# Bringing an expert's gathered rows to the places of the block transposes: by way of DRAM, or by 16 direct transfers on the chip

## The chip, the cores and the metric

The kernel runs on one core of one Trainium2 chip. The metric is the device time of one execution in microseconds (us); the times shown are medians of several runs. TensorE (PE) multiplies matrices and loads their weights (PEld), VectorE (DVE), ScalarE (ACT) and GpSimd (POOL) do the rest of the arithmetic, and SyncE (SP) only issues transfers. Sixteen DMA engines carry out the transfers of all queues.

## The reference, cut to what matters

The input is 2048 tokens of 512 numbers (batch 8, sequence 256). A first layer adds to x a long convolution over `ctx` gated by the normalised x. The second layer, where the change lies, is a mixture of experts:

```python
x = hidden_states.reshape(-1, h)                       # 2048 tokens of 512, normalised
scores = softmax(x @ gate_w.T)                         # 16 experts
topk_w, topk_i = top_k(scores, 4)                      # 4 experts a token, weights made to sum to 1
...                                                    # each expert takes at most CAP = 256 tokens
xg = xpad[buf]                                         # (16, 256, 512): every expert's gathered rows
mid = silu(xg @ w_gate) * (xg @ w_up)                  # 512 -> 352
eout = (mid @ w_down) * wbuf                           # 352 -> 512
y = zeros(T + 1, h).at[buf].add(eout)                  # added back to the tokens' rows
shared = silu(x @ sw_gate) * (x @ sw_up) @ sw_down     # 704 wide, for all tokens
out = x + y + shared
```

## The kernel before, in words

All arithmetic is float32. The order of the instructions on each engine is the order in which the Python code writes them; each engine and each queue works in that order. The framework puts in the semaphore waits that the data need.

The first half of the time (to about 340 us) is the convolution layer. Between its steps the kernel places pieces of the shared MLP: `shared_block` is a generator, and `fill(n)` runs its next n pieces on PE. A piece multiplies into a PSUM tile `sgu` (two buffers, tag `mm`); ACT makes `act` of it and DVE multiplies both into `smid` (L179). The last shared blocks run from 357 to 419 us, while the experts' routing is worked out on DVE and POOL.

Then 16 experts run one after the other. For expert e:

- `find` (L915) turns the routing into two lists of 128 row numbers, `ido` to gather by and `idx` to scatter by.
- `gather(e)` (L974) is two indirect DMAs on POOL. They bring 256 rows of `xw_d` (512 numbers and 16 weights each) from DRAM into the tile `g`, laid out [128 partitions, 2 halves of the list, 528]. `g` has two buffers.
- `shuffle(g)` (L985) makes `gb` of `g`. DVE's transpose works on blocks of 32 x 32, so to get the transposed matrix the rows' 32-row groups j and the 128-column groups i have to change places: what stands in partitions 32j to 32j+31 and columns 128i to 128i+127 of `g` is wanted in partitions 32i to 32i+31, at place j of `gb`. The kernel before does that in DRAM: one store of the 512 KB (L989), a wait until it landed, and four fetches of 128 KB (L992), all on SP. `gb` has two buffers.
- `tokens(e)` (L998) copies the weights `wg` out of `g` and transposes `gb` into `xgT` with two DVE instructions (L404).
- `gate_up` (L1023) and `down` (L1076) are the matmuls: 24 groups of gate and up (`pgu`, lines 1034, 1046, 1054), then for each half of the list the down projection (`eo`, L1080). `down` also scales the result on DVE and adds it to `out` by an indirect DMA on POOL (L1091).
- `load_expert` (L852) issues four weight loads on SP, 2112 KB in all.

The experts are prepared three ahead (`AHEAD = 3`). Gathers and shuffles of experts 0, 1 and 2 are issued before the loop, among the last shared blocks. In the loop, `tokens(e + 1)` comes behind the gate and up matmuls of e, and at the end of expert e SP gets the weights and the shuffle of e + 3:

```python
        if e + AHEAD < E:
            experts[e + AHEAD] = load_expert(e + AHEAD)
            moved[e + AHEAD] = shuffle(gathered[e + AHEAD])
```

So SP works through four weight loads and one shuffle for each expert, in this order, and what waits in one of them holds up all behind it. SP also carries the stores of `out` (L196) that the shared blocks end with.

Of the kernel before, what the change touches and what calls it, by code (L numbers as in the profile page):

```python
# [8 lines left out]
F32 = mybir.dt.float32  # L9
# [11 lines left out]
P = 128  # L21
BK = 32
B, S, L = 8, 256, 512
# [7 lines left out]
E, K, CAP, I, IS = 16, 4, 256, 352, 704  # L31
NSL = CAP // P
NB = P // BK
# [20 lines left out]
def ssm_attention__then__moe_kernel(  # L54
# [22 lines left out]
    nc = tc.nc  # L77
# [7 lines left out]
    dram = ctx.enter_context(tc.tile_pool(name="dram", bufs=1, space=DRAM))  # L85
# [52 lines left out]
    def transpose_blocks(dst, got):  # L138

        nc.vector.transpose(dst, got.rearrange("p j (c f) -> p c j f", f=BK))  # L140
# [119 lines left out]
    with ExitStack() as att:  # L260
# [16 lines left out]
            out=exch,  # L277
            in_=exch,
# [386 lines left out]
        def stir(count):  # L665
# [7 lines left out]
            out=skip_b,  # L673
            in_=bass.AP(tensor=skip.tensor, offset=skip.offset + FIRST * HT, ap=[[0, P], [1, HT]]),
# [164 lines left out]
    ffn = ctx.enter_context(tc.tile_pool(name="ffn", bufs=2))  # L839
# [6 lines left out]
    AHEAD = 3  # L846
# [138 lines left out]
    def shuffle(g):  # L985


        slots = dram.tile([CAP, L], F32, name="slots", bufs=2)
        nc.sync.dma_start(out=slots.rearrange("(n q) f -> q n f", n=NSL), in_=g[:, :, 0:L])  # L989
        gb = ffn.tile([P, NSL * NB, P], F32, name="gb", bufs=AHEAD - 1)  # L990
        for i in range(NB):
            nc.sync.dma_start(  # L992
                out=gb[i * BK : (i + 1) * BK],
                in_=slots[:, i * P : (i + 1) * P].rearrange("(j b) f -> b j f", b=BK),
            )
        return gb

    def tokens(e):  # L998

        gb, g = moved.pop(e), gathered.pop(e)  # L1000
        wg = ffn.tile([P, NSL], F32, name="wg")
        for n in range(NSL):
            nc.vector.tensor_copy(wg[:, n : n + 1], g[:, n, L + e : L + e + 1])
        xgT = ffn.tile([P, NC, CAP], F32, name="xgT")
        for n in range(NSL):
            transpose_blocks(xgT[:, :, n * P : (n + 1) * P], gb[:, n * NB : (n + 1) * NB])
        return xgT, wg

    NW, Q = I // P, P // 4
# [99 lines left out]
    for e in range(AHEAD - 1):  # L1109
        gathered[e] = gather(e)  # L1110
        moved[e] = shuffle(gathered[e])
    fill(6)
    xgT_next = tokens(0)
    wt_next = pack(experts[0][0])
    gathered[AHEAD - 1] = gather(AHEAD - 1)
    moved[AHEAD - 1] = shuffle(gathered[AHEAD - 1])
    while behind:
        fill(1)
    for e in range(E):
        w, wd = experts.pop(e)  # L1120
        wt = wt_next
        xgT, wg = xgT_next
        mid = ffn.tile([P, NI, CAP], F32, name="mid")
        if e + 1 < E:
            gate_up(xgT, mid, w, wt, slice(0, CAP))
            wt_next = pack(experts[e + 1][0])
            xgT_next = tokens(e + 1)
            if e + AHEAD < E:
                find(e + AHEAD, hots.pop(e + AHEAD))
                gathered[e + AHEAD] = gather(e + AHEAD)  # L1130
            for n in range(NSL):
                down(e, n, mid, wd, wg)
            if e + AHEAD + 1 < E:
                hots[e + AHEAD + 1] = compare(e + AHEAD + 1)
        else:

            gate_up(xgT, mid, w, wt, slice(0, P))
            gate_up(xgT, mid, w, wt, slice(P, CAP), (NW,))
            down(e, 0, mid, wd, wg)
            gate_up(xgT, mid, w, wt, slice(P, CAP), range(NW))  # L1140
            down(e, 1, mid, wd, wg)
# [3 lines that stand above are left out]
# [38 lines left out]
```

## Time and profile before

| | |
|---|---|
| median of 3 runs | 678.43 us (678.39 to 678.44) |
| the profiled execution | 678.52 us |
| its span, first to last instruction | 676.8 us |
| mean granted TensorE clock | 0.995 |
| DMA packets | 98439, 117.79 MB |

The span is what the tables of the profile cover; the profiled execution's own time lies 1.7 us over it. A share of busy time tells how full an engine is on average; which wait ends last in a stage has to be read from the chain of waits, the waits and the timeline of that stage. SP's entries are issues: their length is the time that the queue's sequencer took, not that of the transfer.

### The profile page before, as it was taken

The numbers are of one execution on the slowest core, as the hardware profiler recorded it, in microseconds if no ns is written. First come the engines' busy times: TensorE is split into PE (matmuls) and PEld (weight loads), VectorE is DVE, ScalarE is ACT, GpSimd is POOL, SyncE is SP. The second block draws the span as 40 slices with busy tenths as digits, with TensorE's granted clock in tenths as the row PEclk, the third lists the DMA queues.
The fourth block names the chain that finished last, engine by engine and source line by source line (L and its number), as shares of the span: only waits on it lengthen the run. The fifth ranks groups of instructions, "written<-read, shape, count | busy, mean of one in ns | idle before, by whom it ended". The sixth has DMA issues, their size and how long they took to land.

```text
span 676.8 us, 9807 instructions
## 1 busy us (share of the span) xinstructions
PE 654.2 (97%) x3321; PEld 486.9 (72%) x3321; DVE 385.8 (57%) x932; ACT 184.2 (27%) x465; POOL 320.2 (47%) x509
## 2 busy tenths in 40 slices
PE   6899999998999999999999999999999999999994
PEld 5687877777867877876867685777776667777772
DVE  4956576878877776767536621444445545553231
ACT  2464533444342343313332010111121111111110
POOL 5677646877685777547120320243333444443111
PEclk9999999999999999999999999999999999999998
DMA  5793455555557536351008672588888889999822
GB/s 131 237 269 105 125 151 145 145 140 140 147 141 188 134 94 161 103 133 46 16 23 298 198 234 64 169 267 255 259 269 269 256 258 270 271 266 273 248 32 31
DMA packets 98439, 117.79 MB, mean 174 GB/s; under 512 B 11268, under 2 KB 64356, under 8 KB 98389
## 3 DMA queue, kind: packets, MB, share of 16 engines
q1 hardware_dynamic: 90932, 99.86, 48.9%
q0 software_dynamic: 7168, 17.04, 12.1%
q10 hardware_dynamic: 288, 0.26, 0.3%
q8 instruction: 26, 0.43, 0.3%
q14 instruction: 25, 0.20, 0.1%
HBM read 84.25 MB, written 32.88 MB: 173 GB/s over the span
## 4 chain that ended last, share of the span: by engine, by line
PE 85%; DVE 4%; DMA 3%; issue 2%; POOL 2%; ACT 2%; SPq 1%; POOLq 0%; DVEq 0%; ACTq 0%
PE sgu L168 20%; PE pgu L1034 15%; PE y L468 15%; PE eo L1080 12%; PE so L185 11%; PE pgu L1054 4%; PE pgu L1046 2%; PE sgt L154 2%; PE shared L468 2%; PE ip L920 1%; PE pt L529 1%; POOL kv L445 1%; DMA xs<-in_x 1%; DMA out<-eo_sb,idx 1%; DVE y L517 1%
## 5 line engine op out<-in xcount | busy, mean ns | idle before, releaser
L468 PE MATMUL y<-kv,toep 128*128 128x288 f32 x528 | 138.7, 407 | 4.8 <-DVE f L518 3.0
L468 PEld LDWEIGHTS y<-kv,toep 128*128 128x128 f32 x528 | 98.9, 190 | 35.4 <-issue 7.1
L977 POOL DMA_INDIRECT g<-xw_d,ido x32 | 34.9, 1092 | 170.8 <-DVE idx L943 132.3
L520 POOL TENSOR_TENSOR f<-f 128x256 f32<-128x256 f32 x60 | 43.8, 730 | 90.2 <-DVE f L518 85.0
L445 POOL TENSOR_TENSOR kv<-k 128x256 f32<-128x256 f32 x126 | 85.1, 707 | 0.0
L1091 POOL DMA_INDIRECT out<-eo_sb,idx x32 | 59.5, 1859 | 46.1 <-DVE eo_sb L1088 35.4
L168 PE MATMUL sgu<-xnT,swg 128*128 128x256 f32 (+1 forms) x400 | 78.1, 338 | 0.4 <-DVE tail L162 0.4
L1034 PE MATMUL pgu<-xgT,w 128*128 128x256 f32 (+1 forms) x384 | 78.2, 362 | 0.0
L168 PE MATMUL sgu<-xnT,swu 128*128 128x256 f32 (+1 forms) x400 | 77.9, 338 | 0.0
L1034 PEld LDWEIGHTS pgu<-xgT,w 128*128 128x128 f32 x384 | 68.2, 190 | 8.7 <-issue 0.5
L185 PE MATMUL so<-swd,smid 128*128 128x512 f32 x160 | 73.9, 593 | 0.0
L168 PEld LDWEIGHTS sgu<-xnT,swg 128*128 128x128 f32 x400 | 65.3, 191 | 7.9 <-DVE tail L162 0.6
L168 PEld LDWEIGHTS sgu<-xnT,swu 128*128 128x128 f32 x400 | 64.6, 191 | 6.3
L1080 PE MATMUL eo<-wd,mid 96*128 96x512 f32 (+1 forms) x132 | 59.4, 598 | 0.0
L1042 DVE TENSOR_TENSOR mid<-eact,pgu 128x256 f32<-128x256 f32 (+1 forms) x34 | 13.8, 406 | 77.6 <-ACT eact L1041 77.6
L491 DVE TENSOR_TENSOR y<-y,again 128x576 f32<-128x576 f32 x28 | 21.4, 766 | 57.8 <-PE y L468 48.1
L185 PEld LDWEIGHTS so<-swd,smid 128*128 128x128 f32 x160 | 29.9, 190 | 31.9 <-issue 30.4
L177 ACT ACTIVATE act<-sgu 128x256 f32<-128x256 f32 (+1 forms) x50 | 17.1, 341 | 121.6 <-PE sgu L168 121.6
L518 DVE TENSOR_TENSOR f<-y,z 128x512 f32<-128x512 f32 x64 | 44.3, 692 | 6.6 <-DVE y L517 0.5
L517 DVE TENSOR_TENSOR y<-y,q 128x512 f32<-128x512 f32 x64 | 44.8, 700 | 2.2
L1063 ACT ACTIVATE eact<-pgu 32x128 f32<-32x128 f32 x32 | 8.5, 267 | 129.0 <-PE pgu L1054 123.8
L1080 PEld LDWEIGHTS eo<-wd,mid 96*128 96x128 f32 (+1 forms) x132 | 24.1, 189 | 26.0 <-issue 23.5
(178 smaller groups left out, 928.2 us busy)
## 6 DMA issues: line engine op xcount, KB each, us to landing
toep<-win_d SPq DMA_DIRECT2D x28, 320.0 KB
slots<-g SPq DMA_DIRECT2D x16, 512.0 KB
gb<-slots SPq DMA_DIRECT2D x64, 128.0 KB
w<-in_L_ffn_w_gate SPq DMA_DIRECT2D x11, 704.0 KB
w<-in_L_ffn_w_up SPq DMA_DIRECT2D x11, 704.0 KB
got<-sent SPq DMA_DIRECT2D x26, 256.0 KB
wd<-in_L_ffn_w_down SPq DMA_DIRECT2D x11, 512.0 KB
xs<-in_x SPq DMA_DIRECT2D x16, 256.0 KB
```

Of the source, the lines that this page charges most:

```text
L168: nc.tensor.matmul(pgu[:, k, :], lhsT=sw[:, c, f * P : (f + 1) * P], rhs=toks[:, c, :], start=(c == 0), stop=(c == NC - 1),)
L185: nc.tensor.matmul(po, lhsT=m[:, i * P : (i + 1) * P], rhs=swd[:, (f - 1) % (NF + 1), :], start=(f == 0), stop=(f == NF),)
L445: (nc.vector if c in helped else nc.gpsimd).tensor_mul(kv[:, c, 0 : ND * HB].rearrange("p (d w) -> p d w", d=ND), kh[:, c, 0:HB].unsqueeze ...
L468: nc.tensor.matmul(out, lhsT=toep[:, m * P : (m + 1) * P], rhs=rhs, start=(n == 0), stop=(n == len(pairs) - 1),)
L517: nc.vector.tensor_mul(yd, yd, view(qq, 0, [[qc, 2], [B, ND], [1, HB]]))
L518: nc.vector.tensor_add(f, yd, z[:, :, :, BACK : BACK + HB])
L520: adder.tensor_add(f[:, :, 0:2, :], f[:, :, 0:2, :], f[:, :, 2:4, :])
L977: nc.gpsimd.indirect_dma_start(out=g[:, n, :], out_offset=None, in_=xw_d[:, :], in_offset=bass.IndirectOffsetOnAxis(ap=ido[:, e, n : n + 1 ...
L1034: nc.tensor.matmul(pgu[:, k, cols], lhsT=w[:, k, c, f * P : (f + 1) * P], rhs=xgT[:, c, cols], start=(c == 0), stop=(c == NC - 1),)
L1054: nc.tensor.matmul(pgu[:, 0, cols], lhsT=wt[:, c, 0:P], rhs=xgT[:, c, cols], start=(c == 0), stop=(c == NC - 1),)
L1080: nc.tensor.matmul(po, lhsT=mid[:m, f, n * P : (n + 1) * P], rhs=wd[:m, f, :], start=(k == 0), stop=(k == NW),)
L1091: done = nc.gpsimd.indirect_dma_start(out=out, out_offset=bass.IndirectOffsetOnAxis(ap=idx[:, e, n : n + 1], axis=0), in_=o, in_offset=Non ...
```

## The change

`shuffle` no longer makes the tile `slots` in DRAM. For each of the four row groups j and four column groups i it issues one transfer on SP that reads 32 partitions of `g` and writes 32 partitions of `gb`: two runs of 512 bytes for each partition, 32 KB in all. `gb` gets one dimension more, [128, 2, 4, 128] in place of [128, 8, 128], and `tokens` indexes it so. The bytes in `gb` and their places are the same.

```diff
     def shuffle(g):
-        slots = dram.tile([CAP, L], F32, name="slots", bufs=2)
-        nc.sync.dma_start(out=slots.rearrange("(n q) f -> q n f", n=NSL), in_=g[:, :, 0:L])
-        gb = ffn.tile([P, NSL * NB, P], F32, name="gb", bufs=AHEAD - 1)
-        for i in range(NB):
-            nc.sync.dma_start(
-                out=gb[i * BK : (i + 1) * BK],
-                in_=slots[:, i * P : (i + 1) * P].rearrange("(j b) f -> b j f", b=BK),
-            )
+        gb = ffn.tile([P, NSL, NB, P], F32, name="gb", bufs=AHEAD - 1)
+        for j in range(NB):
+            for i in range(NB):
+                nc.sync.dma_start(
+                    out=gb[i * BK : (i + 1) * BK, :, j, :],
+                    in_=g[j * BK : (j + 1) * BK, :, i * P : (i + 1) * P],
+                )
         return gb
...
-            transpose_blocks(xgT[:, :, n * P : (n + 1) * P], gb[:, n * NB : (n + 1) * NB])
+            transpose_blocks(xgT[:, :, n * P : (n + 1) * P], gb[:, n])
```

## The prediction

> **What bounds the kernel now.** I read the page first, for which engine has no idle time left.
>
> ```profile
> span 676.8 us, 9807 instructions
> PE 654.2 (97%) x3321; PEld 486.9 (72%) x3321; DVE 385.8 (57%) x932; ACT 184.2 (27%) x465; POOL 320.2 (47%) x509
> PE   6899999998999999999999999999999999999994
> DMA  5793455555557536351008672588888889999822
> ```
>
> TensorE is full from end to end; but in the last third, where the experts run, the 16 DMA engines stand at 8 and 9 tenths too. So two things can decide: TensorE, and whether data still comes in time. The chain of waits in order of time shows one expert like the next (start, length, step):
>
> ```profile
> 605.28 1.02 PE pgu L1046 x16
> 606.31 1.92 PE pgu L1054 x8
> 608.23 6.91 PE pgu L1034 x32
> 615.52 5.26 PE eo L1080 x12
> 620.78 1.02 PE pgu L1046 x16
> ```
>
> 15.50 us per expert; the 0.38 between 615.14 and 615.52 is `find`'s matmuls, so no step waits. The table of windows agrees: in 605 to 620 PE is busy 15.00 of 15.00 us with the DMA share at 0.94. The waits, of the engines and of SP's queue, say who waits for the code that is replaced:
>
> ```profile
> DVE xgT L404 <- DMA gb<-slots: 1.5, 1, 1.5
> SPq L992 <- DMA slots<-g: 111.3, 15, 11.3
> SPq L860 <- DMA w<-in_L_ffn_w_up: 1.5, 1, 1.5
> ```
>
> The big number, 111.3 us, is SP itself, holding the fetches until the store landed. No compute engine pays for it, save DVE once, 1.5 us before the first expert, and PE did not stop there. The third line is a limit to keep in mind: a weight load at 366.78 waited for the landing of another weight load, issued at 360.38, eight SP transfers earlier. An SP issue waits for the one eight before it.
>
> Last the timeline, at the only place where DVE waited, and through one later cycle of SP:
>
> ```profile
> 390.31 0.38 SPq L989 DMA_DIRECT2D slots<-g  x1
> 393.55 1.81 SPq L992 DMA_DIRECT2D gb<-slots  x4
> 397.69 1.31 DVE L404 STREAM_TRANSPOSE xgT<-gb 128x512 f32<-128x512 f32 x2 [1.49 <-DMA gb<-slots]
> 399.11 0.42 DVE L179 TENSOR_TENSOR smid<-act,sgu 128x256 f32<-128x256 f32 x1
> 401.94 1.89 PE L168 MATMUL sgu<-xnT,swg 128*128 128x256 f32 x8
> ...
> 591.65 0.38 SPq L859 DMA_DIRECT2D w<-in_L_ffn_w_gate  x1
> 592.08 0.43 SPq L860 DMA_DIRECT2D w<-in_L_ffn_w_up  x1
> 592.61 0.43 SPq L861 DMA_DIRECT2D wd<-in_L_ffn_w_down  x1
> 593.08 0.77 SPq L864 DMA_DIRECT2D wd<-in_L_ffn_w_down  x1
> 593.96 0.56 SPq L989 DMA_DIRECT2D slots<-g  x1
> 605.90 1.80 SPq L992 DMA_DIRECT2D gb<-slots  x4
> 607.80 0.48 SPq L859 DMA_DIRECT2D xs<-in_L_ffn_w_gate  x1
> ```
>
> **Own time.** The profiled execution took 678.52 us, 1.7 outside its span of 676.8, and 0.09 over the median 678.43. Changes are added to the median.
>
> **Part 1: what goes.** Per expert one store and four fetches, and SP's wait between them. Compute paid only DVE's 1.5 us, under which PE kept running: worth 0. The waits cannot pay off at the end either: SP's last fetches are issued at 636.37, and from there to PE's end at 667.3 no PE step waits.
>
> **Part 2: what comes, on SP.** 16 issues of 32 KB instead of 5. No row shows a transfer from on-chip memory to on-chip memory. The nearest are 12 transfers of 64 KB in a row, over 32 partitions in 512-byte runs, kp out, got in, qp out: from 124.82 to 130.51, 0.474 us each. Sixteen are 7.6 us. Bounds: 0.40 (the first issues of other groups) and 0.6 (issues of 256 KB), so 6.4 to 9.6; I take 7.6.
>
> **Part 3: on the DMA engines.** In 395 to 397.4 queue q1 used 89.7% of 16 engines for 1069 packets, nearly all 512-byte fetches: 32 ns a packet. In 124.8 to 126.4, kp's stores, 268 packets at 34.0%: also 32 ns. The expert's 1024 pieces thus cost 1024 x 32 / 16 = 2.1 us by either side's row, 4.1 if reading and writing on chip add up. Gone are fetches of 2.1 and the store: 71.3% over 391.5 to 393.6, 1.5 us. So the DMA load of 0.94 x 15.5 = 14.6 us per expert goes to 13.1, or at worst 15.1. Below 15.5 in both cases; I take 13.1, since two rows give the same price.
>
> **Part 4: the first expert.** SP starts at 390.31 (the gathered rows are there), so the 16th issue is at 390.31 + 15 x 0.474 = 397.4. From the last old fetch (393.55 + 3 x 0.474 = 395.0) to DVE's start it was 2.7 us, so DVE starts about 400.1, not 397.69. Queued behind the waiting transposes on DVE is `smid`, the product of a shared block: it frees a PSUM buffer that PE's matmuls at 401.94 need (two buffers). 400.1 + 1.31 + 0.11 + 0.42 = 401.94: just in time. So the cover of about 2.4 us that `smid` had is used up: cost 0 to 0.4, taken 0.2; at an issue pace of 0.6 it is 401.94 + 15 x 0.13 = 1.9 late. Also POOL's gather for expert 2 (396.47) now waits for the reads of `g`, to about 400; its rows are due at 445. The out stores behind on SP (401.03) slip some 5 us; the first scatter on `out` is at 434.86. Moves for experts 1 and 2 end by about 414, in time for the next SP issue at 414.92. All hidden.
>
> **Part 5: the experts in the loop.** SP's cycle: the old one ran (636.37 - 443.05) / 12 = 16.1 us, 0.6 over PE's 15.5. It could, because the first in-loop fetches were issued by 444.88 and due at 461.28: the lead shrank, and is still 8.3 us at the end (638.27, due 646.57). New cycle: weights issued 0 to 2.3, four moves to 4.2, then the eight-back rule holds: moves 5 to 8 follow as the four weight loads land, 9 to 16 as moves 1 to 8 land. Old store and weights drained by 14.25 us (591.65 to 605.90), 13.1 at 607.80. Without the old fetches ahead (2.1, against about 1.0 of late moves) and with 0.5 of moves in place of the store's 1.5, that is about 11 to 12; then 8 x 0.474 = 3.8: a cycle of 15 to 16. Worst, nothing gained: 13.4 + 3.8 = 17.2. The lead allows 461.28 - 2.7 - (437.95 + 7.6) = 13 us over 12 cycles, 1.1 each: break-even is 16.6. I take 15.5 to 16, cost 0.
>
> The rows above show 12 small transfers overlapping at 0.474 us each. The Trainium skill, "DMA: Bandwidth & Descriptors" (Rules for kernel authors), speaks against the change: coalesce small transfers, since under 64 KB one pays mostly overhead, a fixed time that it puts near 2 us for transfers that GpSimd issues. By that price paid in turn, 16 moves would be 32 us, an estimate by which SP's cycle would be twice PE's and the kernel some 200 us slower. The trace does not bear it out where transfers overlap.
>
> Sum: 678.43 + 0 + 0.2 + 0 = 678.6. About 0.2%, 1.36 us, is what a measurement of this kernel can tell from no change.
>
> **Rivals.**
> *SP's cycle becomes the bound (slower).* For it: the eight-back rule, 20 issues where 9 were, a DMA share of 0.94. Against it: less DMA work, and a 13 us lead. Its place is the wait of `xgT` for `gb` in late experts; it decides from a cycle of 16.6. At 17.2: 12 x 1.7 - 13 = 7.4 late, 686.
> *The first expert's moves stall a shared block (slower).* At a pace of 0.6, or one issue held up 1.7 as in fetches at 407.16 (3.06 us for four): 1.4 to 2, so 680.3.
> *It does not do what it says:* pieces for different `j` interleave in the same partitions; were each held behind the last one there, four rounds of about 2.7 would come after the weights: a cycle of 13.4 + 3 x 2.7 = 21.5, 12 x 6 - 13 = 59 late, 737. Against it: `swt`'s two interleaved halves, at 17.36 and 18.01, were issued with no wait between.
> *Faster:* the DMA relief shortens something at the end. But only 668 to 676.8 is free of PE, with no SP transfer near it; at most some tenths through the last scatter, or 1.5 if the first matmuls had stood behind DVE: 677.
>
> **How the numbers follow.** No change 0.56; first-expert stall 0.17; SP's cycle 0.20; ordered pieces 0.03; faster 0.04. Slower is 0.40. The range starts at 678.0, a little under the first case, and ends at 687, past the first-expert stall and past SP's case at 17.2; what it leaves out is the faster case, the ordered one and longer cycles. The likeliest case alone: 678.2 to 679.4.
>
> **What would show it.** Right: in the waits the 111.3 us of SP at the store are gone; PE is 15.00 of 15.00 in windows of the expert stage; the DMA share there falls from 0.94 to about 0.85; DVE's `xgT` waits once, about 4 us, near 396 to 400. Wrong: `xgT L404 <- DMA gb<-g` among DVE's waits for several experts, PE idle at `pgu L1046`, an issue pace over 0.6 or SP's cycle over 16.6.

## The result, and the profile after

The kernel with direct moves takes 679.84 us (median of 20 runs, 678.10 to 680.29) against 678.41 us before (20 runs on the same chip, 678.18 to 678.58). By the medians it is 1.43 us slower, 0.21%; the ratio is 1.0019, with a 95% interval of [1.0012, 1.0026]. That is at the bound of 0.2% that the prediction named, and clear of no change. The profiled execution took 680.24 us, 1.7 outside its span again. Of the 20 times, 17 lie between 679.66 and 680.29 and three between 678.10 and 678.35; the profiled one belongs to the many.

The page, for the same four rows as before:

```profile
span 678.5 us, 10053 instructions
PE 655.6 (97%) x3321; PEld 487.7 (72%) x3321; DVE 386.2 (57%) x932; ACT 184.2 (27%) x465; POOL 319.7 (47%) x509
PE   7899999998999999999999999999999999999994
DMA  5794455555556535441018632677899999999822
```

The span grew by 1.7 us. TensorE is as full as it was, and the DMA row has not become lighter: eight nines in a row where there were four. The waits (total, times, longest):

```profile
PE sgu L168 <- DVE smid L179: 1.4, 1, 1.4
SPq L991 <- DMA g<-xw_d,ido: 11.8, 3, 4.9
DVE xgT L404 <- DMA gb<-g: 5.6, 1, 5.6
```

SP's 111.3 us at the store's landing are gone, as the change promised. The moves wait for their gathered rows only three times, once before the loop (4.4 us) and for experts 3 and 4 in it (2.5 and 4.9). In the loop they also wait for weight loads to land, up to 1.7 us at a time, as the prediction said of transfers issued eight places ahead. In exchange `xgT` waits 5.6 us, once, and there is a wait of TensorE, 1.4 us, that the kernel before did not have. The timeline shows where (SP's 32 issues are those of experts 0 and 1):

```profile
390.26 22.03 SPq L991 DMA_DIRECT2D gb<-g  x32
401.94 1.31 DVE L404 STREAM_TRANSPOSE xgT<-gb 128x512 f32<-128x512 f32 x2 [5.61 <-DMA gb<-g]
403.17 0.71 DVE L179 TENSOR_TENSOR smid<-act,sgu 128x256 f32<-128x256 f32 x2
403.60 1.99 PE L168 MATMUL sgu<-xnT,swg 128*128 128x256 f32 x8 [1.37 <-DVE smid L179]
```

SP begins to issue at 390.26, as before, but expert 0's rows are on their places only at 401.94. DVE stands before the two transposes until then, with `smid` queued behind them. `smid` was done at 399.53 before; here the first is done only near 403.6, and PE, which needed its PSUM buffer at 401.94 in the old trace, stops for 1.37 us. The chain of waits names the same steps, and what comes behind:

```profile
400.08 1.84 DMA gb<-g
401.94 1.31 DVE xgT L404 x2
403.24 0.32 DVE smid L179
403.60 7.17 PE sgu L168 x32
...
421.08 1.02 PE pgu L1045 x16
...
607.04 1.02 PE pgu L1045 x16
...
622.54 1.02 PE pgu L1045 x16
```

The first matmul of expert 0 starts at 421.08, 1.77 us later than before (419.31; 0.12 of this was there at 389.98 already, ahead of the moves), and from there the experts follow at 15.50 us each, as before. So the whole loss arises before 421, and neither the loop nor the end adds to it. In the window 607 to 622 (us, then busy time of PE, PEld, DVE, ACT and POOL, the clock, the DMA share and GB/s) PE has no gap:

```profile
607.00:622.00 15.00, 15.00 (x85) 11.01 (x84) 7.69 (x19) 2.49 (x7) 5.65 (x6) 1.00 0.96 252
```

The DMA engines move 252 GB/s there against 284 before, yet their share is 0.96, not lower than 0.94.

What one issue costs stands in the source view of line 991 (least, median and most, in ns):

```profile
L991 SPq DMA_DIRECT2D gb<-g x256: 585/595/1927, 390.3 to 642.5; - x128
```

About 0.59 us, and 0.04 more to the next: 0.64 a move. Sixteen take 10.4 us (390.26 to 400.67), where the old store, wait and fetches took 5.1.

### The profile page after: what moved, and what is told of

The parts are those of the page before. It is cut to its first block, busy times and chain, and to the rows that moved or that the text cites. A ratio compares the mean times of both kernels' runs of the same rounds, so it can differ in the third digit from the quotient of the medians.

```text
span 678.5 us, 10053 instructions
## 1 busy us (share of the span) xinstructions
PE 655.6 (97%) x3321; PEld 487.7 (72%) x3321; DVE 386.2 (57%) x932; ACT 184.2 (27%) x465; POOL 319.7 (47%) x509
## 2 busy tenths in 40 slices
DMA packets 97160, 109.42 MB, mean 161 GB/s; under 512 B 14084, under 2 KB 67172, under 8 KB 97109
## 3 DMA queue, kind: packets, MB, share of 16 engines
q1 hardware_dynamic: 89652, 91.48, 46.3%
q0 software_dynamic: 7168, 17.04, 14.0%
## 4 chain that ended last, share of the span: by engine, by line
PE 81%; DMA 5%; DVE 4%; POOL 2%; issue 2%; SPq 2%; ACT 2%; POOLq 0%; DVEq 0%; ACTq 0%
PE sgu L168 17%; PE pgu L1033 15%; PE y L468 14%; PE eo L1079 12%; PE so L185 10%; PE pgu L1053 4%; PE pgu L1045 2%; PE shared L468 2%; PE sgt L154 1%; SPq L991 1%; DMA xw_d<-prob 1%; PE pt L529 1%; PE ip L920 1%; POOL kv L445 1%; DMA xs<-in_x 1%
```

## The experiments

My theory: all of the loss is expert 0's 16 moves, which at 0.64 us an issue land after the point where DVE's wait is free. The rival: the loss is a change in the loop or elsewhere on the chip, such as the DMA engines' share, and the wait at 403 only one visible part of it.

### The moves of one expert alone

**first_dram** is after with the old way for expert 0 alone; **first_direct** is before with the moves for expert 0 alone.

```diff
+        if e == 0:          # first_dram; "e > 0" in first_direct
+            slots = dram.tile([CAP, L], F32, name="slots", bufs=2)
+            ...             # the store and four fetches of before
+            return gb
         for j in range(NB):
             for i in range(NB):
```

> After, but expert 0 alone goes by way of DRAM again (one store, four fetches); experts 1 to 15 keep the 16 direct moves. Theory A (the whole 1.4 us is PE's stall at 402 us, where DVE waits for expert 0's moves with smid queued behind it): back to 678.4, within 0.3. Theory B (the cost lies in the loop, in SP's longer cycle or in contention on the DMA engines): stays at 679.8.

> The reverse: expert 0 alone by 16 direct moves, all others by way of DRAM. Theory A: 679.8, the full loss, with PE idle about 1.4 us before L168 at 402 to 404. Theory B: 678.4.

first_dram took 678.27 us (677.95 to 678.44), ratio 0.9998 [0.9989, 1.0007]: the loss is gone, with 240 of 256 moves still there. DVE's timeline:

```profile
398.72 1.30 DVE L404 STREAM_TRANSPOSE xgT<-gb 128x512 f32<-128x512 f32 x2 [2.59 <-DMA gb<-slots]
```

first_direct took 680.21 us (678.40 to 680.37), ratio 1.0023 [1.0014, 1.0032]: 16 moves bring the whole loss, with the same stop of TensorE (timeline, PE):

```profile
403.32 1.99 PE L168 MATMUL sgu<-xnT,swg 128*128 128x256 f32 x8 [1.18 <-DVE smid L179]
```

So in these runs the moves of experts 1 to 15 cost nothing, and those of expert 0 cost everything.

### The same moves with a later due time, or an earlier start

**late_tokens** is after with expert 0's transposes two pieces of the shared block later.

```diff
-    fill(6)
+    fill(8)
     xgT_next = tokens(0)
```

> After, with the transposes of expert 0 placed two pieces of the shared block later on DVE (fill(8) in place of fill(6) before tokens(0)), so that one more smid goes ahead of them. All 16 moves of all experts stay. Theory A: 678.4, since nothing that PE needs is queued behind the wait. Theory B: 679.8.

678.17 us (677.90 to 678.43), ratio 0.9998 [0.9989, 1.0007]. All 256 moves are there; they land no sooner, but `smid` now stands ahead of the transposes in DVE's order (timeline, DVE):

```profile
398.81 0.42 DVE L179 TENSOR_TENSOR smid<-act,sgu 128x256 f32<-128x256 f32 x1 [3.03 <-ACT act L177]
...
401.65 1.30 DVE L404 STREAM_TRANSPOSE xgT<-gb 128x512 f32<-128x512 f32 x2 [2.29 <-DMA gb<-g]
```

The transposes start at 401.65, practically as late as in after, and it costs nothing. What hurt was not their lateness but what stood behind them. The time cannot be told from before's.

**early_prob** lets `prob`'s store, for which the first gather waits, be issued ahead of expert 2's weight loads.

```diff
-    experts = {e: load_expert(e) for e in range(AHEAD)}
+    experts = {e: load_expert(e) for e in range(AHEAD - 1)}
...
     nc.sync.dma_start(out=xw_d[0:T, L:ROW].rearrange("(n q) e -> q n e", q=P), in_=prob)
+    experts[AHEAD - 1] = load_expert(AHEAD - 1)
```

> After, with the weights of expert 2 issued on SP behind the store of prob and not ahead of it, so that prob lands some 6 us earlier and POOL's first gather no longer starts at 382.5 to 383, where it took 2.4 to 2.9 us beside DVE's 2.28 us `hot` (the other gathers: 0.95). Of 20 runs of after 3 took 678.1 to 678.35 and 17 took 679.66 to 680.29. Theory A (the stall at 402 us hangs on when expert 0's rows land; the two kinds of run are a first gather ahead of `hot` or beside it): every run at 678.2 to 678.4, no stall. Rival (the two kinds come from SP's issue pace, whatever the gather does): most runs still at 679.8.

678.15 us (678.03 to 679.38), ratio 0.9996 [0.9988, 1.0005]: gone again. The moves start at 385.81 and the transposes at 397.97, and PE does not stop there. The profiled run is the one at 679.38, and what it has over the other ten comes late in the loop (waits):

```profile
DVE xgT L404 <- DMA gb<-g: 19.9, 7, 3.8
```

Six of the seven waits are those of experts 10 to 15. SP's cycle, from one expert's first weight load to the next, was 16.8 us in this run ((633.72 - 448.73) / 11), over the prediction's break-even of 16.6, and the last experts start 16.00, 15.30 and 15.23 us apart (605.03, 621.03, 636.33, 651.56) where before had 15.50, 15.02 and 15.01: 1.0 us in all. That is the prediction's first rival in small. Why the cycle was longer in this run is open. early_prob also showed something about the gather, to which the last experiments come back.

### What sets the pace of an issue

0.64 lay above my upper bound of 0.6. **pace** adds 32 unused transfers of 32 KB to before, in groups of four: a, chip to chip like a move (32 partitions, two runs of 512 bytes); b, chip to DRAM; c, DRAM to chip; d, chip to chip with one run of 1 KB.

```diff
+    for k, here in enumerate(quarters):
+        nc.sync.dma_start(out=to_a[here], in_=g2[quarters[k - 1], :, 0:P])
+    ...                                        # to_b, to_c, to_d, and all once more
```

> Before, with 32 unused transfers of 32 KB added on SP after the shuffle of expert 2, where SP is idle: four of a kind, twice over. Kinds: a) on chip to on chip, two runs of 512 bytes for each of 32 partitions, like the moves; b) on chip to DRAM, same shape; c) DRAM to on chip, same shape; d) on chip to on chip, one run of 1024 bytes. The moves were issued 0.64 us apart, where 0.474 was expected. If both ends on the chip make the difference: a and d 0.64, b and c 0.47. If the shape with two runs does: a, b and c 0.64, d 0.47. The total says nothing here.

One run, 678.43 us. SP's timeline, four issues a row:

```profile
411.81 2.51 SPq L1127 DMA_DIRECT2D to_b<-g  x4
414.36 2.50 SPq L1130 DMA_DIRECT2D to_c<-xw_d  x4
416.91 2.49 SPq L1132 DMA_DIRECT2D to_d<-g  x4
419.44 2.57 SPq L1125 DMA_DIRECT2D to_a<-g  x4
```

0.63 to 0.64 for all four: neither having both ends on the chip nor having two runs a partition is by itself the reason. Both branches of what I expected fell. **pace2** varies size and runs, all from the chip to DRAM: e, 32 partitions with four runs of 512 bytes, 64 KB; f, 32 with one run of 2 KB; h, 128 with one of 512 bytes; i, 32 with four of 256 bytes, 32 KB; j, 32 with two of 2 KB, 128 KB.

```diff
+        nc.sync.dma_start(out=to_e[k, :, :, 0:P], in_=g2[here, 0, 0:L].rearrange("p (n f) -> p n f", f=P))
+        ...                                    # to_f, to_h, to_i, to_j
```

> Before, with 20 unused transfers from the chip to DRAM added on SP after the shuffle of expert 2, four of a kind: e) 64 KB, 32 partitions with four runs of 512 bytes; f) 64 KB, 32 partitions with one run of 2 KB; h) 64 KB, 128 partitions with one run of 512 bytes; i) 32 KB, 32 partitions with four runs of 256 bytes; j) 128 KB, 32 partitions with two runs of 2 KB. All four kinds of the run pace were issued 0.64 us apart, wherever their ends lay; kp's stores, 64 KB in four runs, 0.474. If size decides: i 0.64, all others 0.47. If the number of runs in a partition decides (four or more are quick): e and i 0.47, f, h and j 0.64. The total says nothing here.

```profile
409.62 2.57 SPq L1125 DMA_DIRECT2D to_e<-g  x4
412.24 1.99 SPq L1127 DMA_DIRECT2D to_f<-g  x4
414.27 1.88 SPq L1129 DMA_DIRECT2D to_h<-g  x4
416.19 2.48 SPq L1131 DMA_DIRECT2D to_i<-g  x4
418.72 2.51 SPq L1133 DMA_DIRECT2D to_j<-g  x4
```

h goes at 0.47 and f does too after its first; e, i and j at 0.63 to 0.64. Size decides nothing: e and h both have 64 KB in runs of 512 bytes. What divides them is how the two ends are described. In e, i, j, b and c the DRAM end runs together into rows of another count than the chip's end (e: 32 x 4 x 128 numbers on the chip, 128 x 128 in DRAM); in f and h both ends have one shape. **pace3** puts that to the test with four kinds of one size, 32 partitions with two runs of 512 bytes: k, chip to DRAM with equal shapes; o, the same with a contiguous DRAM end; l, DRAM to chip with equal shapes; m, chip to chip as in a move.

```diff
+    to_k = dram.tile([NB, NSL, BK, P], F32, name="to_k")
+    to_o = dram.tile([NB, BK, NSL, P], F32, name="to_o")
+        nc.sync.dma_start(out=to_k[k].rearrange("n b f -> b n f"), in_=g2[here, :, 0:P])
+        nc.sync.dma_start(out=to_o[k], in_=g2[here, :, 0:P])
+        ...                                    # to_l, to_m
```

> Before, with 16 unused transfers behind the gather of expert 2, four of each kind, all of 32 KB in 64 runs of 512 bytes over 32 partitions. k: chip to DRAM, both ends described as 32 x 2 x 128; o: the same to a contiguous place, so that the DRAM end is described as 64 x 128 and the two ends differ in shape; l: DRAM to chip, both ends 32 x 2 x 128; m: chip to chip, both ends 32 x 2 x 128, as the changed kernel's moves. Theory (a transfer with one end in DRAM and both ends of one shape is issued quickly, any other slowly; that is how all kinds measured so far divide): k and l 0.43 to 0.48 us per issue, o and m 0.59 to 0.65. Rival (32 partitions with two runs each are slow wherever they go; nothing measured so far had that shape and was quick): all four 0.59 to 0.65. Time of the kernel within 0.2% of before.

```profile
408.12 2.84 SPq L1124 DMA_DIRECT2D to_k<-g  x4
411.01 2.56 SPq L1126 DMA_DIRECT2D to_o<-g  x4
413.61 1.99 SPq L1128 DMA_DIRECT2D to_l<-xw_d  x4
415.65 2.57 SPq L1130 DMA_DIRECT2D to_m<-g  x4
```

The rows of four hide a first issue each: k's first took 1.43 us and its other three 0.43, 0.42 and 0.43; l's first 0.58 and then 0.42, 0.43 and 0.42; o and m 0.59 to 0.65 throughout. For these transfers the theory holds: an issue is quick (0.43, with the gap 0.47) when one end is in DRAM and both are described by the same shape, and slow (0.59, with the gap 0.64) when the shapes differ or both ends are on the chip. The trace's own records of the issues name the rows of the destination, and agree with this reading: 1 x 128 for e and 1 x 64 for o, but 2 x 32 for k, l and m. Why the issue takes longer, the records don't show. k's one issue of 1.43 us is not explained, and one row of before does not fit: the fourth weight load has one end in DRAM and, by the code, 96 rows of 2 KB at both ends, and yet (source view, ns):

```profile
L864 SPq DMA_DIRECT2D wd<-in_L_ffn_w_down x11: 457/664/1060, 361.4 to 624.7; - x11
```

It comes close behind three other large loads. So something else can lengthen an issue too, which was not tested.

### Where the loop's own limit lies

**moves20** splits four of the 16 moves of experts 3 to 15 in two: 20 issues, the same bytes.

```diff
+                parts = [slice(0, NSL)]
+                if e >= AHEAD and j == 0:
+                    parts = [slice(n, n + 1) for n in range(NSL)]
+                for n in parts:
```

> After, with 4 of the 16 moves of experts 3 to 15 split in two halves of 16 KB: 20 issues in place of 16, the same bytes. Rival of the prediction, SP's cycle: measured 16.15 us in after, with 3 us of it spent waiting for landings. If each issue adds its 0.64: cycle 18.7, 12 x 3.2 less the lead of 12.6 makes 26 us, 706. If the waits take it up: cycle 16.2 to 16.5, below the break-even of 16.55, and 679.8.

701.10 us (699.08 and 703.11), ratio 1.0334 [1.0310, 1.0358]. The waits, and one gap of TensorE in the timeline:

```profile
DVE xgT L404 <- DMA gb<-g: 52.7, 11, 6.3
```

```profile
600.34 1.77 PE L1049 MATMUL pgu<-xgT,wt 128*64 128x128 f32 x16 [2.55 <-DVE xgT L404]
```

The first rival of the prediction, come true: SP's cycle, taken from one expert's first weight load to the next over 11 experts (452.54 to 651.97), is 18.1 us. Above the break-even of 16.6 by 1.5, it makes some 18 us over 12 cycles, to which expert 0's 1.4 comes: 698, where the profiled run took 699.08. Four more issues made the cycle 1.95 us longer, 0.49 each, less than 0.64: a part of SP's waits disappears under them. The changed kernel, at 16.15, is 0.4 us away from this.

### Half of the moves on another queue

**two_queues** gives eight of expert 0's 16 moves to ACT's queue.

```diff
-                nc.sync.dma_start(
+                (nc.scalar if i % 2 and first else nc.sync).dma_start(
```

> After, with expert 0's moves dealt out on two queues, 8 on SP and 8 on ACT; all else as after. Theory A (it is the issue time of 16 moves in one queue, 16 x 0.64): the last move is issued near 395 and landed by 397, PE does not stall, 678.3. Rival (what makes 0.64 is shared by the queues, or the DMA engines are the limit): the moves end as late as before, 679.8.

682.81 us (681.31 to 684.53), ratio 1.0062 [1.0048, 1.0075]: worse than after, which no theory had said. ACT's timeline, and PE's:

```profile
389.65 6.90 ACTq L991 DMA_DIRECT2D gb<-g  x8
396.66 0.38 ACT L161 ACTIVATE act<-sgt 64x256 f32<-64x256 f32 x1 [17.81 <-DMA gb<-g]
```

```profile
397.55 3.68 PE L168 MATMUL sgu<-xnT,swg 128*128 128x256 f32 x8 [2.67 <-DVE tail L162]
```

The moves did land early; the transposes ran at 398.20 without a wait. But eight issues hold ACT for 6.90 us (0.62 each in the source view, 0.86 with the gaps), and the `act` that the shared block waits for stands behind them. The stop of 2.67 us is not all. Behind it the clock that TensorE was granted fell (window 398 to 402, columns as above):

```profile
398.00:402.00 4.00, 4.00 (x13) 3.23 (x12) 1.37 (x4) 0.12 (x1) 1.89 (x2) 0.61 0.45 115
```

At 0.61 the eight matmuls took 3.68 us, where they take 1.89 otherwise; stop and slow matmuls together make the 4.4 us. Behind the stop of 1.37 us in after the clock stayed at 1.00. The Trainium skill, "DMA: Bandwidth & Descriptors" (Issuing engines are not separate DMA queues), calls the time to initiate a transfer usually small relative to the transfer itself. For transfers as small as these the trace does not agree: an issue took 0.59 us on SP and 0.62 on ACT, a third of the 1.84 us from the start of the last issue to expert 0's rows, and ACT's `act` had to wait until all eight were out.

### Why the rows are late in the first place

In after, POOL's first gather of expert 0 takes 2.36 us where the second takes 0.97 (timeline, POOL); in before it was 2.50, so this is nothing that the change brought. It runs beside DVE's comparison `hot` for expert 2 (timeline, DVE):

```profile
383.04 2.36 POOL L977 DMA_INDIRECT g<-xw_d,ido  x1 [27.87 <-DMA xw_d<-prob]
385.70 0.97 POOL L977 DMA_INDIRECT g<-xw_d,ido  x1 [0.30 <-issue]
```

```profile
382.01 2.29 DVE L907 TENSOR_TENSOR hot<-pos,slot_f 128x2048 bf16<-128x2048 f32 x1
```

In early_prob the first gather came when no `hot` ran, and took 1.23 us. **hot_later** and **hot_later2** move that comparison behind more of the shared block:

```diff
     for e in range(1, AHEAD):
+        if e > 1:
+            fill(1)                # fill(2) in hot_later2
         hots[e] = compare(e)
-        fill(3)                    # kept in hot_later
+        fill(4 - e)                # in hot_later2
...
-    fill(6)
+    fill(5)
```

> After, with VectorE's comparison hot for expert 2 (2.29 us, 382.01 to 384.30 in after) put behind one more piece of the shared block (and one piece fewer before expert 0's transposes, so that their place in TensorE's order stays). In after POOL's first gather ran beside that comparison, from 383.04, and took 2.36 us where the second took 0.97. Theory (the gather is held up by VectorE beside it, and expert 0's rows and moves start late for it): the first gather takes 0.95 to 1.25 us, expert 0's moves start some 1.1 to 1.4 us earlier (near 389), the transposes' inputs land at 400.5 to 400.8, TensorE's 1.37 us wait is gone or under 0.3: 678.1 to 678.6. Rival (the gather's long time is of its own or of the stores ahead of it): it takes 2.3 us again, moves start at 390.3, time 679.6 to 680.3. The comparison may in its new place fall beside another gather of expert 0 or 1; beside expert 0's second one the theory gives no gain either.

> As hot_later, whose edit did not reach its aim: there the comparison for expert 2 still ran ahead of the shared block's VectorE work, at 381.54, beside POOL's first gather, which took 2.90 us and ended 1.1 us behind the comparison (384.92 against 383.82; in after 385.40 against 384.30). Here it is put behind two pieces of the shared block instead of one (and one fewer ahead of expert 0's transposes), so that the block's addition xs stands ahead of it in VectorE's order. Theory (a gather beside this comparison waits for it): the first gather takes 0.95 to 1.25 us from about 382, the second follows at once, expert 0's moves start at 387.6 to 388.6 (390.26 in after) and its transposes no longer hold TensorE: 678.0 to 678.5; the comparison now stretches one of expert 1's gathers instead, which nothing waits for. Rival (the first gather is slow by itself, or the rows land late whatever the gather does): moves start near 389.9 again, 679.6 to 680.3.

hot_later missed its aim: `hot` still ran at 381.54, beside the gather, which took 2.90 us. 679.95 us (679.54 to 680.22), ratio 1.0023 [1.0014, 1.0032], so nothing gained. That is the rival's time, but not for the rival's reason: the comparison of expert 3, pushed back to 389.61, made the shared block's `xs` late, and TensorE stopped there and no longer for the transposes at 401.64 (timeline, PE):

```profile
392.55 1.99 PE L168 MATMUL sgu<-xnT,swg 128*128 128x256 f32 x8 [1.15 <-DVE xs L195]
```

hot_later2 took 678.96 us (678.73 to 679.27), ratio 1.0009 [1.0000, 1.0018]. Its POOL, DVE and PE in the timeline:

```profile
382.25 1.23 POOL L979 DMA_INDIRECT g<-xw_d,ido  x1 [27.18 <-DVE idx L943]
386.30 1.89 POOL L979 DMA_INDIRECT g<-xw_d,ido  x1 [0.30 <-issue]
```

```profile
385.04 2.33 DVE L907 TENSOR_TENSOR hot<-pos,slot_f 128x2048 bf16<-128x2048 f32 x1
399.26 1.30 DVE L404 STREAM_TRANSPOSE xgT<-gb 128x512 f32<-128x512 f32 x2 [2.35 <-DMA gb<-g]
```

```profile
392.19 2.00 PE L168 MATMUL sgu<-xnT,swg 128*128 128x256 f32 x8 [0.43 <-DVE xs L195]
```

The first gather takes 1.23 us, the moves start at 387.57 and the transposes at 399.26, 2.7 us earlier than in after, and the wait of 1.37 us is gone. The time falls by 0.9 and not by the 1.4 expected, since the comparison of expert 3, pushed back to 389.25, makes `xs` late and TensorE stops for 0.43 us there. A gather of expert 1 now meets `hot` and ends at 388.19, 0.82 us behind it, as in after (391.09 against 390.27) and in early_prob (385.36 against 384.54). The Trainium skill, "SBUF — State Buffer" (Who interferes with whom), says that a VectorE instruction with two SBUF inputs contends with a GpSimd one that reads SBUF, and calls the ports that they share an exclusive lock. `hot` has two inputs, the gather reads its list of rows, and in all of these runs a stretched gather ends a fixed time behind the comparison, 0.82 us, or 1.10 where it is the first one: the trace agrees.

## Why the prediction was right and wrong, point by point

**The likeliest case, no change within 0.2%,** was missed. By size it lies on the border (1.43 us against a bound of 1.36, but 0.19% by the ratio), and 679.84 is outside the 678.2 to 679.4 given for it; by mechanism it is wrong, since a loss is there and has a place. The range held the result only because it had been drawn to take in the rivals; the sum, 678.6, was 1.24 too low. What happened is the prediction's second rival, the stalled shared block (1.4 to 2 us, given a chance of 0.17), by its mechanism, in its place and at the lower end of its price.

**Part 1** holds. The 111.3 us of SP's waiting were worth nothing, since no compute engine stood behind them.

**Part 2 is the step that failed.** I took 0.474 us an issue, bounds 0.40 to 0.6; it was 0.64, outside the bounds. The row was chosen by size and runs (kp, qp and got: 64 KB in runs of 512 bytes), and the 0.6 of larger issues was put down to their size. Size has no part in it (pace2): the quick rows have one end in DRAM and equal shapes, while both ends of a move are on the chip (pace3, m). A row of before could have told that there are two prices at all, the stores of `out`, whose ends differ in shape, in the source view of line 196 (ns):

```profile
L196 SPq DMA_DIRECT2D out<-xs x16: 537/563/677, 64.9 to 420.1; - x16
```

**Part 4** was right in its mechanism and mis-sized by that term. The last issue came at 400.08 instead of 397.4, 2.7 later; from there to the transposes it took 1.86 us, not 2.7; so DVE started at 401.94 instead of 400.1. With the cover of 2.4 us already spent, as foreseen, the 1.84 of delay became 1.37 of a stopped TensorE where 0.2 was taken. A second error, 0.84 us the other way in the landing, thus hid part of the first: by the prediction's own sum a pace of 0.64 would have been 2.5 late. POOL's gather for expert 2 slipped to 402.82 instead of the 400 foreseen, and nobody waited for it. That this place decides is shown from both sides by first_dram and first_direct, and that the cover is what counts by late_tokens, early_prob and hot_later2.

**Part 5** holds in its verdict for this kernel, with a thinner margin than I gave it. SP's cycle is 16.15 us ((628.21 - 450.53) / 11), over the 15.5 to 16 that I took, 0.4 under the break-even, and no shorter than before's 16.16 by the same count ((622.78 - 444.99) / 11). The lead at the end, from the landing of the last row by the trace's semaphore updates to the transposes, was 3.8 us (644.56 to 648.37). Before it was 3.5 by the same count (643.03 to 646.57); the 8.3 of the prediction ran from the end of the last issue, so it made the old lead too long. Part of the 3.8 is owed to expert 0's delay: in the versions without it 1.8 (first_dram) and 2.0 (late_tokens) were left, and in early_prob's profiled run nothing. moves20 shows that four issues more fall over the edge: the first rival was near. SP's timeline of one cycle:

```profile
613.10 0.52 SPq L859 DMA_DIRECT2D xs<-in_L_ffn_w_gate  x1
615.67 12.43 SPq L991 DMA_DIRECT2D gb<-g  x16
628.21 0.54 SPq L859 DMA_DIRECT2D w<-in_L_ffn_w_gate  x1
```

Sixteen issues of 0.64 are 10.2 of the 12.43 us; only the rest is waiting.

**Part 3** was wrong. The bytes fell (109.42 MB in all, from 117.79), and the share of the DMA engines in the expert stage did not fall to 0.85 but stayed at 0.94 to 0.96. The page's rows of the queues tell part of it. SP's queue fell from 48.9% to 46.3% of the engines' time over the run. The queue of POOL's gathers and scatters moved the same packets and bytes in more time (packets, MB, share; before, then after):

```profile
q0 software_dynamic: 7168, 17.04, 12.1%
q0 software_dynamic: 7168, 17.04, 14.0%
```

A packet's time in the records thus isn't work alone, and a sum of packets times a price does not give the share. The prediction's own worst case, 15.1 us of 15.5 if reading and writing on the chip add up, would be 0.97; no run here decides whether that is the reason. What sets the share stays open. It cost nothing in after, as nobody waited for it.

**Ordered pieces** and **faster** did not show. The Trainium skill's rule to coalesce, as weighed in the prediction, would have had some 200 us by its 2 us a transfer; the runs put the price of a small overlapping transfer at its issue, 0.47 or 0.64 us.

One thing stays open: three of the 20 runs of after, and one of the 11 of first_direct, were as quick as before. hot_later2 and early_prob suggest that in these the gather got ahead of the comparison, but no such run was profiled, so it is not shown.

## What to carry to other kernels

Replacing one large transfer by many small ones trades a landing for issue time: count the issues, price them by a row whose two ends are described like yours, and ask first where the *first* use is due, since a queue that keeps up in the loop may still be late at its start. Look what stands behind the waiting instruction: one line that changes the order (late_tokens) won back everything without making the data any earlier.

## What the runs showed of the hardware that I had not expected

- SP issued the test transfers in 0.43 us when one end was in DRAM and both ends had one shape, and in 0.59 us otherwise, whatever the size (32 to 128 KB) or the runs (256 bytes to 2 KB). In the kernel the fourth weight load does not fit (0.46 to 1.06 us). ACT took 0.62 us for each of eight moves, 0.86 with the gaps.
- An indirect DMA on POOL that meets a two-input comparison of DVE (2.29 us) ends 0.8 to 1.1 us behind it: 1.59 to 3.06 us instead of 0.95 to 1.23.
- With 11% fewer GB/s moved in the same stage (252 against 284), the DMA engines' share stayed at 0.96 (0.94 before), and the same 7168 packets of POOL's queue took 14.0% of the engines' time instead of 12.1%.
- Behind a stop of 2.67 us TensorE was granted 0.61 of its clock in the window 398 to 402 (two_queues), behind one of 1.37 us all of it (after, 403 to 406).
